# A graph network layer on one core: the order of the last table stores, the register loads and one late-turned group

## The chip, the cores and the metric

The kernel runs on one core of a Trainium2 chip. The metric is the device time of one execution in microseconds. A profiled execution is slower than the ones that are timed; it is used to see what happens, and the timed runs to say how long it takes.

## The reference

There are N = 6250 nodes with H = 128 features and E = 100000 edges, sorted by destination, with four attributes each. Everything is float32.

```
msg_in     = concat([x[src], x[dst], edge_attr], axis=1)      # E x 260
h          = silu(msg_in @ mW1 + mb1)                          # E x 128
messages   = h @ mW2 + mb2
aggregated = segment_sum(messages, dst)                        # N x 128
u          = silu(concat([x, aggregated]) @ uW1 + ub1)
updated    = u @ uW2 + ub2
r          = layer_norm(x + updated) * ln_g + ln_b
out        = normalize(x + r)                                  # a second norm, without weights
```

## The kernel before

**Tables.** The first matmul is split by the rows of mW1. A table A = x @ mW1[:128] and a table B = x @ mW1[128:256] + mb1 are computed once for all nodes and stored to HBM as tab_a and tab_b. This is the prologue's loop (from L367): the nodes come in seven parts k = 0 to 6 of eight tiles of 128 (part 6 has one tile, so its two stores have 64 KB, the others 512 KB). In each part TensorE turns the next part of x (turn_x, L336), multiplies (L377), ScalarE copies A out of PSUM (L379), VectorE adds the bias to B (L380), and SyncE stores first A (L383), then B (L384). Each part's last matmul is kept in the list `table`. The PSUM tiles come from a pool of four, all called "wide". A tile with zeros fills the rows of B behind the last node (L332 to L334).

**Edges.** The edges come in NG = 98 groups g of 1024 edges, eight tiles of 128. For each group:

- fetch(g) (L273): GpSimd gathers the rows of the edges' sources with one indirect DMA per tile (L277), up to eight of 64 KB per group. Groups 0 to 4 (below RAW = 5) gather from x itself, because A is not ready; the later ones from tab_a. A gather can be told to wait for matmuls named in the call: `fetch(4, *table[3:])` makes the first half of group 4 wait for the last matmul of part 3, the second half for that of part 4. The gathered rows lie in six buffers, so group 6 needs the buffer of group 0.
- load(g) (L598): SyncE loads mv, the 96 rows of B from the group's base node on (L604, with the base in a register of SyncE), and st, the four attribute rows of ea_d (L605). Every fourth group it also loads `near` for four groups from near_d (destinations, L315).
- node_matrix(g) (L607): VectorE makes a one-hot matrix of destinations in the upper 96 rows of st.
- products(g) (L632): TensorE multiplies st by mv (L636). For groups below RAW the gathered rows of x must be multiplied by mW1 too (L639), and for that they have been turned (transposed) before, by turn_rows (L357): eight transposes on TensorE and one copy of 128x1024 on VectorE (L362).
- hidden(g) (L645): VectorE adds the gathered rows of A and the products (L653, not for groups below RAW), ScalarE takes silu (L654).
- by_nodes(g) (L670): TensorE sums the edges by node with a second one-hot matrix (L665); add(g) (L676) adds the result on VectorE at the group's base, which needs the base in a register of VectorE.

Each engine works through its own queue in the order in which the code is written. In iteration g of the loop (L693) stand load(g+4), hidden(g), products(g+2), node_matrix(g+3), edge_matrix(g+1), add(g-2), by_nodes(g) and a fetch. The fetches of the start are fetch(5) behind turn_rows(2), with no matmul to wait for in its first half; fetch(6) with its second half behind products(0); fetch(7) and (8) in iterations 0 and 1; fetch(9) in iteration 3 behind products(4) and (5). From g = 12 on, group g+2 is fetched in iteration g, its second half behind the first sum of group g.

**What the change touches.** load_bases(g) (L343) loads the bases of 14 groups into registers of both SyncE and VectorE; it is called at k = 4 for the first 14. At k = 4 stand also fetch(4), destinations(0) and turn_rows(1). After the parts, groups 2, 3 and 4 are turned (L404 to L406), a tile `pad` of zeros is made and stored behind the last attribute in ea_d (L407 to L410), and the pools of the tables are closed. The buffers stbuf (L596) take memory that the tables had.

Of the kernel before, what the change touches and what calls it, by code (L numbers as in the profile page):

```python
# [8 lines left out]
F32 = mybir.dt.float32  # L9
# [5 lines left out]
ENG = mybir.EngineType  # L15
PSUM = bass.MemoryType.PSUM
DRAM = bass.MemoryType.DRAM

P = 128
# [5 lines left out]
def kernel(  # L25
# [40 lines left out]
    nc = tc.nc  # L66
    N, H = x.shape
# [3 lines left out]
    NP = NT * P  # L71
# [38 lines left out]

    tables = ExitStack()
    tpool = tables.enter_context(tc.tile_pool(name="tables", bufs=1, side="right"))
    tables_ps = tables.enter_context(tc.tile_pool(name="tables_ps", bufs=4, space=PSUM))

    def wide():
        return tables_ps.tile([P, G, P], F32, name="wide")

    def narrow():
        return wide()[:, :2, :].rearrange("p i f -> p (i f)")
# [148 lines left out]
    rows, bases, near = {}, {}, {}  # L268

    def tiles_of(g):  # L270
        return min(G, -(-(E - g * GE) // P))
# [57 lines left out]
    def by_node(t):  # L329
        return t[:NP].rearrange("(i p) f -> p i f", p=P)  # L330

    zeros = tpool.tile([W, H], F32, name="zeros")  # L332
    nc.vector.memset(zeros, 0.0)
    nc.sync.dma_start(tab_b[NP:NW], zeros)  # L334

    def turn_x(i0, n):  # L336
        pt = wide()
# [2 lines left out]
        nc.scalar.copy(xT[:, i0 * P : (i0 + n) * P], pt[:, :n, :].rearrange("p i f -> p (i f)"))  # L340
        return ins

    def load_bases(g):  # L343
        _, vals = nc.values_load_multi_w_load_instructions(
            base_i[0:1, g : g + RB],
            engines=(ENG.SP, ENG.DVE),
            min_val=0,
            max_val=NP,
            skip_runtime_bounds_check_because=IN_RANGE,
        )  # L350
        for k, v in enumerate(vals):
            bases[g + k] = v

    parts = groups(NT, G)
    table = []

    def turn_rows(g):  # L357

        px = wide()
        for i in range(G):  # L360
            ins = nc.tensor.transpose(px[:, i, :], rows[g][:, i, :], ident)
        nc.vector.tensor_copy(rows[g], px)  # L362
        return ins
# [3 lines left out]
    for k, (i0, n) in enumerate(parts):  # L367
        if k + 1 < len(parts):
            turn_x(*parts[k + 1])

        tb = x_sb[:, i0 : i0 + n, :]
        ta = tpool.tile([P, G, H], F32, name="t", bufs=2)
        for j0, m in groups(n, G // 2):
            pm = wide().rearrange("p (i s) f -> p i s f", s=2)
            for j in range(m):
                cols = slice((i0 + j0 + j) * P, (i0 + j0 + j + 1) * P)
                ins = nc.tensor.matmul(pm[:, j], xT[:, cols], w1, start=True, stop=True)  # L377
            own = slice(j0, j0 + m)
# [4 lines left out]
        nc.sync.dma_start(by_node(tab_a)[:, i0 : i0 + n, :], ta[:, :n])  # L383
        nc.sync.dma_start(by_node(tab_b)[:, i0 : i0 + n, :], tb)  # L384
# [12 lines left out]
        cols = slice(i0 * P, NW if i0 + n == NT else (i0 + n) * P)  # L397
        nc.vector.memset(acc[:, cols], 0.0)
        if k == 4:
            fetch(4, *table[3:])  # L400
            destinations(0)
            load_bases(0)
            turn_rows(1)
    fetch(RAW, None, turn_rows(2))  # L404
    for g in range(3, RAW):
        turn_rows(g)  # L406
    if E < NG * GE:  # L407
        pad = tpool.tile([ED, NG * GE - E], F32, name="pad")
        nc.vector.memset(pad, 0.0)
        nc.sync.dma_start(ea_d[:, E:], pad)  # L410
    tables.close()

    fixed = edges.enter_context(tc.tile_pool(name="fixed", bufs=1, space=PSUM))
# [8 lines left out]
    def node_y():  # L422
        return node_ps.tile([P, BT, H], F32, name="y")
# [171 lines left out]
    nodes = edges.enter_context(tc.tile_pool(name="nodes", bufs=1))  # L595
    stbuf = [held.tile([K1, GE], F32, name=f"st{k}") for k in range(NST)]  # L596

    def load(g):  # L598

        if g % NQ == 0 and g:  # L600
            destinations(g)
        if g % RB == 0 and g:
            load_bases(g)
        nc.sync.dma_start(mv[g % NM][:W], tab_b[bass.ds(bases[g], W), :])  # L604
        nc.sync.dma_start(stbuf[g % NST][W:], ea_d[:, g * GE : (g + 1) * GE])  # L605

    def node_matrix(g):  # L607

        nc.vector.tensor_scalar(  # L609
            stbuf[g % NST][:W],  # L610
            near.pop(g),
            p_next,
            0.0,
            op0=OP.is_equal,
            op1=OP.add,
            accum_out=deg_q[g // DQ % 2][:, g % DQ * 32 : g % DQ * 32 + 1],
        )
# [13 lines left out]

    def products(g):  # L632
        pre = rows_ps()
        st = stbuf[g % NST].rearrange("k (i c) -> k i c", i=G)
        for i in range(tiles_of(g)):
            ins = nc.tensor.matmul(pre[:, i, :], st[:, i, :], mv[g % NM], start=True, stop=g >= RAW)  # L636
            begun.setdefault(g, ins)
            if g < RAW:
                ins = nc.tensor.matmul(  # L639
                    pre[:, i, :], rows[g][:, i, :], w1[:, 0, :], start=False, stop=True  # L640
                )
            ended[g] = ins
        return pre
# [26 lines left out]
    def by_nodes(g, h, oh):  # L670

        pt = degrees(g)
        sums(g, pt, h, oh, 0, tiles_of(g))
        return pt

    def add(g, pt):  # L676
        at = acc[:, bass.ds(bases[g], W)]
        nc.vector.tensor_add(at, at, pt[:, :W])  # L678
        if g % DQ == 0:
            for k in range(min(DQ, NG - g)):  # L680
                row = slice(32 * k, 32 * k + 1)
                at = deg[row, bass.ds(bases[g + k], W)]
                nc.vector.tensor_add(at, at, pt[row, W:])  # L683

    for g in range(LEAD):
        load(g)
# [5 lines left out]
    fetch(6, None, ended[0])  # L692
    for g in range(NG):  # L693
        if g == 1:
            load_weights()
        if g == 2:
            running.append(destination_checks(node_y()))
        if g == 8:
            running.append(fuse_weights())
        for c in range(1, NC):  # L700
            if g == max(1, c * EC // GE - 10):
                attributes(c)
            if g == max(1, c * EC // GE - 10) + 1:
# [12 lines left out]
        if g - 2 in pt:  # L716
            add(g - 2, pt.pop(g - 2))
        if last:
            break
        pt[g] = by_nodes(g, h.pop(g), oh.pop(g))  # L720
        if CLOSE <= g + 2 < NG:
            fetch(g + 2, begun[g + 2], summing[g])
        elif g == 0:
            fetch(7, ended[1], begun[2])
        elif g == 1:
            fetch(8, begun[3], summing[1])
        elif g % 2:
            fetch(g // 2 + 8, ended[g + 1], begun[g + 2] if g == CLOSE - 3 else ended[g + 2])
        if g >= NG - 3:
            add(g - 1, pt.pop(g - 1))  # L730
        for i0, n, first in batches[:-1]:
            if g == (first if first >= NG - 3 else first + 1):
                fine = i0 == batches[-2][0]
                running.append(node_batch(i0, n, *node_tiles(nodes, node_y), fine=fine))
        for _ in range(0 if g == NG - 2 else 4 if g == NG - 3 else 2 if g >= NG - 6 else 1):
            advance(running)
        if g == NG - 3:
            final = node_batch(
                *batches[-1][:2],
                nodes,  # L740

                lambda name, p=P: gath.tile([P, G, H], F32, name="ga")[:p, :BT],
                lambda: rows_ps()[:, :BT],
                final=True,
            )
            next(final)
        if g == NG - 2:
            next(final)
# [195 lines left out]
```

## Time and profile before

| | us |
|---|---|
| median of three timed runs | 1005.5 |
| lowest and highest of them | 1005.47, 1007.06 |
| the profiled execution | 1170.27 |
| its span, from the first to the last instruction | 1168.2 |

| engine | busy us | share of the span |
|---|---|---|
| TensorE matmuls | 741.4 | 63% |
| TensorE weight loads | 672.5 | 58% |
| VectorE | 486.6 | 42% |
| ScalarE | 238.1 | 20% |
| GpSimd | 742.1 | 64% |

The TensorE clock that was granted in the profiled execution is 0.673 in the mean. In a timeline a line gives the start in us, the duration in us, the engine (PE is TensorE, DVE VectorE, ACT ScalarE, POOL GpSimd, SPq the queue of DMAs that SyncE issues), the line of the code, the operation, what it writes and reads, and in brackets how long the engine was idle before and what ended that. A DMA's line covers its issue, not its transfer. In a table by stretches each row gives the stretch, its length, busy time with a count of instructions for PE, weight loads, DVE, ACT and POOL, the granted clock, the share of the DMA engines and GB/s. In the page's list of groups a line ends with busy time and mean ns, and behind the second bar the idle time before it.

### The profile page before, as it was taken

To read this page: it belongs to the slowest core of one execution; us is meant where nothing else is said; L and a number is where in the kernel's file an instruction comes from. 1 tells how busy PE (TensorE), PEld (TensorE's weight loads), DVE (VectorE), ACT (ScalarE), POOL (GpSimd) and SP (SyncE) were. 2 spreads that over 40 slices of the span, in tenths; PEclk is the share of its full clock that TensorE was granted. 3 is DMA by queue.
4 is the path that set the end of the run, shared out by engine and by line. 5 is a ranking of instruction groups with operands and counts; after the bars stand their busy time and mean duration, and the time that the engine had idled before them with its cause. 6 is when DMAs were issued, how large, how long until landed. Compare 5 with 4: busy or idle time off the path is not lost.

```text
span 1168.2 us, 11310 instructions
## 1 busy us (share of the span) xinstructions
PE 741.4 (63%) x3645; PEld 672.5 (58%) x3645; DVE 486.6 (42%) x1019; ACT 238.1 (20%) x296; POOL 742.1 (64%) x790
## 2 busy tenths in 40 slices
PE   5776886665666667647656756676566555764663
PEld 4665775655655565546555655665465545664552
DVE  4461754432523532542443343353252343254354
ACT  1210121220311120221121122032121113022233
POOL 6646666666666566656666666666666666666661
PEclk9777887666577567666666666566656766656677
DMA  8762232232222231223132223232322222222220
GB/s 197 202 162 71 76 83 63 67 82 63 72 67 74 56 80 51 74 70 82 48 83 60 70 59 82 63 80 59 76 66 71 73 59 68 70 53 65 55 70 25
DMA packets 70076, 89.01 MB, mean 76 GB/s; under 512 B 20703, under 2 KB 51694, under 8 KB 70010
## 3 DMA queue, kind: packets, MB, share of 16 engines
q0 software_dynamic: 25024, 51.30, 17.9%
q1 hardware_dynamic: 40408, 35.03, 10.4%
q10 hardware_dynamic: 4578, 1.89, 0.7%
q8 instruction: 31, 0.51, 0.2%
q14 instruction: 35, 0.29, 0.1%
HBM read 76.78 MB, written 11.38 MB: 75 GB/s over the span
## 4 chain that ended last, share of the span: by engine, by line
issue 34%; PE 31%; POOL 23%; DVE 2%; another core or an unknown queue 2%; DMA 1%; ACT 1%; DVEq 0%; POOLq 0%; SPq 0%; ACTq 0%
POOL ga L277 23%; PE pre L636 15%; PE pt L665 12%; PE y L533 1%; DMA ga<-tab_a,src_i 1%; PE pre L639 1%; PE y L524 1%; PE y L510 1%; PE y L514 0%; PE y L518 0%; DVE s L653 0%; PE pt L660 0%; ACT L654 0%; DVE st L483 0%
## 5 line engine op out<-in xcount | busy, mean ns | idle before, releaser
L277 POOL DMA_INDIRECT ga<-tab_a,src_i x742 | 702.7, 947 | 384.5 <-issue 204.1
L636 PE MATMUL pre<-mv,st 100*128 100x128 f32 x1564 | 342.1, 393 | 228.3 <-issue 200.6
L636 PEld LDWEIGHTS pre<-mv,st 100*128 100x128 f32 x1564 | 312.6, 298 | 248.5 <-issue 228.6
L665 PE MATMUL pt<-oh,h 128*128 128x96 f32 x1564 | 293.6, 346 | 149.2 <-issue 148.0
L665 PEld LDWEIGHTS pt<-oh,h 128*128 128x128 f32 x1564 | 279.4, 264 | 166.5 <-issue 164.4
L653 DVE TENSOR_TENSOR s<-ga,pre 128x1024 f32<-128x1024 f32 x92 | 112.2, 1220 | 500.5 <-DMA ga<-tab_a,src_i 425.5
L654 ACT ACTIVATE h<-s 128x1024 f32<-128x1024 f32 x92 | 97.1, 1056 | 665.0 <-issue 438.8
L609 DVE TENSOR_SCALAR_CACHE_REDUCE st<-near,p_next 96x1024 f32<-96x1024 uint8 x98 | 124.3, 1269 | 3.1 <-DMA near<-near_d 1.5
L622 DVE TENSOR_TENSOR oh<-w_row,rel 128x768 f32<-128x768 f32 x98 | 93.0, 949 | 42.1 <-remote 34.3
L535 DVE TENSOR_TENSOR y<-y,xs 128x512 f32<-128x512 f32 (+1 forms) x12 | 8.3, 688 | 79.1 <-issue 76.1
L277 POOL DMA_INDIRECT ga<-in_x_dram,src_i x32 | 30.7, 959 | 16.5 <-issue 8.5
L654 ACT ACT_TABLE_LOAD x23 | 29.5, 1283 | 24.2 <-PE pre L639 17.7
L377 PE MATMUL wide<-w,xT 128*128 128x256 f32 x98 | 29.0, 460 | 6.1 <-DVE x_sb L380 6.1
L489 ACT ACT_TABLE_LOAD x24 | 30.8, 1283 | 6.1 <-DVE mv L484 5.7
L521 ACT ACTIVATE uT<-y,ub_col 128x512 f32<-128x512 f32 (+1 forms) x12 | 8.1, 678 | 105.9 <-remote 74.5
L377 PEld LDWEIGHTS wide<-w,xT 128*128 128x128 f32 x98 | 22.7, 238 | 10.7 <-DVE x_sb L380 6.8
L533 PEld LDWEIGHTS y<-u,uT 128*128 128x128 f32 x94 | 22.7, 327 | 10.2 <-issue 10.2
L678 DVE TENSOR_TENSOR acc<-acc,pt 128x96 f32 x98 | 23.7, 242 | 5.3 <-remote 4.5
L533 PE MATMUL y<-u,uT 128*128 128x128 f32 x94 | 25.2, 416 | 0.0
L683 DVE TENSOR_TENSOR deg<-deg,pt 1x96 f32 x98 | 24.4, 249 | 1.0
L639 PE MATMUL pre<-w,ga 128*128 128x128 f32 x80 | 19.7, 326 | 4.5 <-issue 4.3
L524 PE MATMUL y<-ub_row,ones 1*128 1x512 f32 (+1 forms) x24 | 14.9, 704 | 8.8 <-ACT uT L521 8.8
(118 smaller groups left out, 358.3 us busy)
## 6 DMA issues: line engine op xcount, KB each, us to landing
ga<-tab_a,src_i POOLq DMA_INDIRECT x742
near<-near_d SPq DMA_DIRECT2D x24, 384.0 KB
mv<-tab_b SPq DMA_DIRECT2D x98, 48.0 KB
tab_a<-t SPq DMA_DIRECT2D x6, 512.0 KB
tab_b<-x_sb SPq DMA_DIRECT2D x6, 512.0 KB
xs<-in_x_dram SPq DMA_DIRECT2D x11, 256.0 KB
out_dram<-z SPq DMA_DIRECT2D x11, 256.0 KB
st<-ea_d SPq DMA_DIRECT2D x98, 16.0 KB
```

Source lines behind the costliest of these rows:

```text
L277: ins = nc.gpsimd.indirect_dma_start(out=rows[g][:, i, :], out_offset=None, in_=x if g < RAW else tab_a[:, :], in_offset=bass.IndirectOffs ...
L377: ins = nc.tensor.matmul(pm[:, j], xT[:, cols], w1, start=True, stop=True)
L489: nc.scalar.activation(r[:, :n], mv[:, :n, 1], AF.Sqrt, bias=eps)
L524: nc.tensor.matmul(y[:, :n], ones[0:1, :], ub2_row[:, None, :].to_broadcast([1, n, H]), start=True, stop=False,)
L533: nc.tensor.matmul(y[:, i, :], by_p[:, :, i], u2, start=final, stop=final or i == n - 1)
L609: nc.vector.tensor_scalar(stbuf[g % NST][:W], near.pop(g), p_next, 0.0, op0=OP.is_equal, op1=OP.add, accum_out=deg_q[g // DQ % 2][:, g % D ...
L622: nc.vector.tensor_tensor(oh, w_row[:, None, :].to_broadcast([P, G, W]), rel[:, g, :, None].to_broadcast([P, G, W]), op=OP.is_equal,)
L636: ins = nc.tensor.matmul(pre[:, i, :], st[:, i, :], mv[g % NM], start=True, stop=g >= RAW)
L639: ins = nc.tensor.matmul(pre[:, i, :], rows[g][:, i, :], w1[:, 0, :], start=False, stop=True)
L653: nc.vector.tensor_add(s[:, :n], ga[:, :n], ps[:, :n])
L654: nc.scalar.activation(h[:, :n], s[:, :n], AF.Silu)
L665: ins = nc.tensor.matmul(pt[:, :W], h[:, i, :], oh[:, i, :], start=i == 0, stop=i == tiles_of(g) - 1)
```

## The change

Five things, none of which changes the arithmetic:

- The store of B of part 5 is held back until part 6, so the order is A5, A6, B5, B6.
- The zeros behind B and behind the attributes are stored in the prologue's beginning, both from the still zero tile deg. The tiles zeros and pad and their memsets go.
- load_bases is called for one engine at a time: for SyncE at k = 4, for VectorE in iteration 1 of the loop, into a dictionary of its own, which add() reads.
- destinations(0) moves from k = 4 to k = 3, and fetch(4) from k = 4 to k = 5, where it waits for the matmuls of parts 4 and 5.
- Group 4 is no longer turned ahead of the loop but in iterations 0 and 1, in two halves of four tiles, each with a PSUM tile of the node stage. The st buffers of groups 0 and 1 come from the pool "work". The pool of PSUM tiles is closed by itself.

```diff
-    zeros = tpool.tile([W, H], F32, name="zeros")
-    nc.vector.memset(zeros, 0.0)
-    nc.sync.dma_start(tab_b[NP:NW], zeros)
+
+    nc.sync.dma_start(tab_b[NP:NW], deg[:W, :H])
+    if E < NG * GE:
+        nc.sync.dma_start(ea_d[:, E:], deg[:ED, : NG * GE - E])
...
-    def load_bases(g):
+    def load_bases(g, engine, bases):
...
-            engines=(ENG.SP, ENG.DVE),
+            engines=(engine,),
...
-        nc.sync.dma_start(by_node(tab_b)[:, i0 : i0 + n, :], tb)
+        stores.append((by_node(tab_b)[:, i0 : i0 + n, :], tb))
+
+        while stores and k != len(parts) - 2:
+            nc.sync.dma_start(*stores.pop(0))
...
             turn_rows(0)
+            destinations(0)
...
         if k == 4:
-            fetch(4, *table[3:])
-            destinations(0)
-            load_bases(0)
+            load_bases(0, ENG.SP, bases)
             turn_rows(1)
+        if k == 5:
+            fetch(4, *table[4:])
     fetch(RAW, None, turn_rows(2))
-    for g in range(3, RAW):
+    for g in range(3, RAW - 1):
         turn_rows(g)
-    if E < NG * GE:
-        pad = tpool.tile([ED, NG * GE - E], F32, name="pad")
-        nc.vector.memset(pad, 0.0)
-        nc.sync.dma_start(ea_d[:, E:], pad)
+    st_first = [work.tile([P, GE], F32, name="s")[:K1] for _ in range(2)]
+    tables_ps.close()
     tables.close()
...
+    st = {g: st_first[g] if g < 2 else stbuf[g % NST] for g in range(NG)}
...
-            load_bases(g)
+            load_bases(g, ENG.SP, bases)
+            load_bases(g, ENG.DVE, at_bases)
...
-        at = acc[:, bass.ds(bases[g], W)]
+        at = acc[:, bass.ds(at_bases[g], W)]
...
+    def turn_late(g):
+
+        for lo in range(0, G, BT):
+            px = node_y()
+            for i in range(BT):
+                nc.tensor.transpose(px[:, i, :], rows[g][:, lo + i, :], ident)
+            yield
+            nc.vector.tensor_copy(rows[g][:, lo : lo + BT], px)
...
     for g in range(NG):
         if g == 1:
+            load_bases(0, ENG.DVE, at_bases)
             load_weights()
...
+        if g == 0:
+            late = turn_late(RAW - 1)
+            next(late)
         if g + 2 < NG:
             pre[g + 2] = products(g + 2)
...
         pt[g] = by_nodes(g, h.pop(g), oh.pop(g))
+        if g < 2:
+            next(late, None)
```

More of the change, by code (lines that the diff above doesn't have):

```diff
@@ L112 @@
     tpool = tables.enter_context(tc.tile_pool(name="tables", bufs=1, side="right"))
-    tables_ps = tables.enter_context(tc.tile_pool(name="tables_ps", bufs=4, space=PSUM))
+    tables_ps = ExitStack()
+    tables_pool = tables_ps.enter_context(tc.tile_pool(name="tables_ps", bufs=4, space=PSUM))
     def wide():
-        return tables_ps.tile([P, G, P], F32, name="wide")
+        return tables_pool.tile([P, G, P], F32, name="wide")
     def narrow():
@@ L267 @@
     near_d = dram.tile([NG, GE], U8, name="near_d")
-    rows, bases, near = {}, {}, {}
+    rows, near = {}, {}
+    bases, at_bases = {}, {}
     def tiles_of(g):
@@ L354 @@
     parts = groups(NT, G)
-    table = []
+    table, stores = [], []
     def turn_rows(g):
@@ L602, in load @@
         if g % RB == 0 and g:
-            load_bases(g)
+            load_bases(g, ENG.SP, bases)
+            load_bases(g, ENG.DVE, at_bases)
         nc.sync.dma_start(mv[g % NM][:W], tab_b[bass.ds(bases[g], W), :])
-        nc.sync.dma_start(stbuf[g % NST][W:], ea_d[:, g * GE : (g + 1) * GE])
+        nc.sync.dma_start(st[g][W:], ea_d[:, g * GE : (g + 1) * GE])
     def node_matrix(g):
         nc.vector.tensor_scalar(
-            stbuf[g % NST][:W],
+            st[g][:W],
             near.pop(g),
@@ L633, in products @@
         pre = rows_ps()
-        st = stbuf[g % NST].rearrange("k (i c) -> k i c", i=G)
+        st_g = st[g].rearrange("k (i c) -> k i c", i=G)
         for i in range(tiles_of(g)):
-            ins = nc.tensor.matmul(pre[:, i, :], st[:, i, :], mv[g % NM], start=True, stop=g >= RAW)
+            ins = nc.tensor.matmul(pre[:, i, :], st_g[:, i, :], mv[g % NM], start=True, stop=g >= RAW)
             begun.setdefault(g, ins)
@@ L681, in add @@
                 row = slice(32 * k, 32 * k + 1)
-                at = deg[row, bass.ds(bases[g + k], W)]
+                at = deg[row, bass.ds(at_bases[g + k], W)]
                 nc.vector.tensor_add(at, at, pt[row, W:])
+    def turn_late(g):
[5 more added lines that the diff above has]
+            nc.vector.tensor_copy(rows[g][:, lo : lo + BT], px)
     for g in range(LEAD):
```

## The prediction

> **What bounds the kernel now.** I read the page's costliest groups, then GpSimd's own timeline, then the chain of waits at the start, then SyncE's and VectorE's timelines there, then the DMA rate by stretches.
>
> ```profile
> L277 POOL DMA_INDIRECT ga<-tab_a,src_i x742 | 702.7, 947 | 384.5 <-issue 204.1
> L277 POOL DMA_INDIRECT ga<-in_x_dram,src_i x32 | 30.7, 959 | 16.5 <-issue 8.5
> ```
>
> Each gather keeps GpSimd busy 947 ns, and 0.30 us pass before the next can start: 1.25 us. There are 742 + 32 + the 8 of group 0 = 782, so 977.5 us. The first starts at 3.07. The last:
>
> ```profile
> 1146.39 0.94 POOL L277 DMA_INDIRECT ga<-tab_a,src_i  x1 [0.30 <-issue]
> ```
>
> It ends at 1147.3; 20.9 us of tail follow to the span's end at 1168.2. So the profiled span is 3.07 + 977.5 + 20.9 = 1001.5 plus 166.7 us of gaps between gathers, most of them in the loop behind a TensorE at a granted clock of 0.673. The profiled execution took 1170.27, 2.07 more than its span. The median of the runs shown is 1005.5; less 2.07 that is 1003.4, so those runs leave about 2 us for all gaps, perhaps 6 if their tail is 4 us shorter. Hence the loop's stalls are mostly missing from them, GpSimd issues almost without a break, and a microsecond by which the gathers start earlier is a microsecond of the total. That is the assumption on which everything below stands. The gaps that the change can touch lie ahead of the loop:
>
> ```profile
> 59.18 0.94 POOL L277 DMA_INDIRECT ga<-in_x_dram,src_i  x1 [0.30 <-issue]
> 69.81 0.94 POOL L277 DMA_INDIRECT ga<-tab_a,src_i  x1 [9.69 <-DMA tab_a<-t]
> ...
> 78.54 0.95 POOL L277 DMA_INDIRECT ga<-tab_a,src_i  x1 [0.30 <-issue]
> 81.65 0.94 POOL L277 DMA_INDIRECT ga<-tab_a,src_i  x1 [2.16 <-PE pre L639]
> ```
>
> The reader is to see two gates one after the other. Group 5, the first from table A, waits until A has landed (69.81). Group 6 then waits for TensorE's first products, which free its buffer (81.65; without that wait it would start at 69.81 + 10.0 = 79.8). What counts for the total is the later gate. The products start at 73.44, when their operands have landed:
>
> ```profile
> 65.64 3.42 DVE L362 COPY ga<-wide 128x1024 f32<-128x1024 f32 x3
> 69.07 0.35 DVE L409 MEMSET pad<- 4x352 f32 x1
> ```
>
> ```profile
> 64.30 0.38 SPq L384 DMA_DIRECT2D tab_b<-x_sb  x1
> 64.77 1.18 SPq L383 DMA_DIRECT2D tab_a<-t  x1
> 66.00 1.25 SPq L384 DMA_DIRECT2D tab_b<-x_sb  x1
> 69.45 0.31 SPq L410 DMA_DIRECT2D ea_d<-pad  x1
> 70.08 0.36 SPq L604 DMA_DIRECT2D mv<-tab_b  x1
> 70.81 0.27 SPq L605 DMA_DIRECT2D st<-ea_d  x1
> ```
>
> ```profile
> 69.45 1.30 DMA ea_d<-pad
> ```
>
> ```profile
> 57.50:60.00 2.50, 2.50 (x7) 2.02 (x6) 0.65 (x2) 0.00 (x0) 1.89 (x3) 0.50 1.04 307
> 64.50:68.50 4.00, 1.47 (x14) 1.23 (x12) 4.00 (x6) 0.00 (x0) 0.00 (x0) 1.00 0.98 286
> 68.50:69.00 0.50, 0.00 (x0) 0.00 (x0) 0.50 (x1) 0.00 (x0) 0.00 (x0) 0.81 0.28 78
> 69.00:69.50 0.50, 0.00 (x0) 0.00 (x0) 0.49 (x3) 0.00 (x0) 0.00 (x0) 0.50 0.00 0
> ```
>
> (The last two columns are the DMA share and GB/s.) The last stores (A5, B5 of 512 KB, A6, B6 of 64 KB) run at 286 GB/s and are moved by about 68.7. SyncE then issues the pad, which waits for VectorE's three copies and a memset; only then mv for group 0, and its st waits 1.30 us for the pad to land. From the issue of st to the first product are 73.44 - 70.81 = 2.63 us, and from there to group 6 are 8.2.
>
> **The change, part by part.**
>
> *B5 and B6 behind A6.* A6 no longer queues behind 524 KB: 524/286 = 1.83 us earlier. B's own end does not move: the same bytes.
>
> *Pad and zeros stored early, from deg.* Two small DMAs at about 20 us (the zeros' issue there took 0.34), with 20 us of slack; the two memsets (0.17 and 0.35) go. At the end, mv no longer waits for the pad: it can go when B has landed. Transfers stop between 68.5 and 69.0; a store's completion reaches the waiting engine later, so I bound it by 69.2 and 69.9: mv is 0.2 to 0.9 earlier, and I take 0.75 as the rate is nearest to zero at 68.7. st follows mv by 0.37 (71.27 to 71.64 for the next group) instead of 0.73: another 0.36. The Trainium skill, "DMA: Bandwidth & Descriptors" ("Anatomy of one DMA", told there of the GpSimd path), puts about 2.0 us of fixed cost on a DMA, most of it the receipt of the write; by that the pad's wait would be 0.7 us longer than the row's 1.30, and the gain as much larger. The row decides: 0.36.
>
> *near for groups 0 to 3 loaded at k = 3.* 393 KB, or 1.37 us at 286 GB/s, leave the stretch of A4, B4 and A5 (issue at 57.58) for the lull after 48 us, where the rate between 50 and 56 is 44 GB/s. SyncE now waits there for near_d to land; behind it is A4, which in the trace isn't ready before 56.25, so the wait lies in slack. In the profile this buys nothing: transfers stop at 63.5 and A5 is issued at 63.57. But A5 is that late because TensorE ran the matmuls of part 5 at half clock (0.57 over 56 to 63: 6.83 us for 18, against 3.32 of weight loads for 16 at full clock). Without TensorE's stalls A5 would come some 3.4 us sooner, into a queue that is full until 63, and then the 1.37 count in full. The timed runs have few of those stalls, so I count 1.37; the other end is 0.
>
> *Gathers of group 4 behind table[4] and table[5].* The second half moves from 55.4 to after the last matmul of part 5, about 62.8, and ends at 68. A5 to B6 now share the engines with it. The Trainium skill, same page, section "Issuing engines are not separate DMA queues", says that transfers of all engines run on the same 16 and interleave; this speaks against the change. By it alone 262 KB cost 262/286 = 0.92 us on B. The row of 57.5 to 60, stores with gathers beside them, has 307 GB/s against 286 without: gathers ask for 65.5 KB per 1.25 us, 52 GB/s, of which 21 came on top, so 60% displaces: 0.55 us on B, 0.4 on A (three gathers). I take the row. GpSimd is free for group 5 at 68.0, before A has landed in any of the cases in which A6 gains under 1.8; if it gains more, everything there is earlier with it.
>
> *Registers apart.* VectorE's loads at k = 4 are the 1.85 us "issue" ahead of the copy at 59.99. They move to g = 1, where VectorE has gaps (9.16 busy of 12 us from 68 to 80) and node matrix 4 waits 1.46 us for near anyway. Behind them are node matrix 4 and edge matrix 2, needed by products 4 and sums 2, over 8 us later. Nothing, both ways, as long as TensorE's queue is behind: at worst 1.85.
>
> *Group 4 turned in the loop; st of groups 0 and 1 in work.* One of three copies (1.14) leaves VectorE's queue ahead of the loop; with the pad and the registers that is 3.3 us, so node matrix 0 (70.96 to 72.24) moves clear of the operands. Eight transposes go into the first two iterations: 8 x 0.116 (2.78 for 24) = 0.93 us of TensorE, and two half copies on VectorE. TensorE is some ten microseconds ahead of the gathers' gates there: group 8 is due at 81.65 + 20 and needs products 3. Cost nothing; if that cover is gone, 0.93 and more (third rival).
>
> **Sum.** First gate, table A: 1.83 + 1.37 - 0.4 = 2.8 earlier. Second gate, products 0: 0.75 + 0.36 + 1.37 - 0.55 = 1.93 earlier. Before, the second was later by 81.65 - 79.8 = 1.85; after, by 2.7. So **the second gate decides and the gain is 1.9 us**: against the profiled execution 1170.27 - 1.9 = 1168.4 if its stalls stayed as they were, which I don't expect; against the median **1003.5 us**. The ends of the terms give 0.0 (near 0, mv 0.2, gathers -0.55) to 2.5 (pad by the longer wait).
>
> **The rivals.**
>
> 1. *The products are not the gate in the timed runs.* TensorE's own rows begin the last matmuls of products 0 at 79.70, well over a microsecond before their release shows; the 0.43 us per two matmuls are half clock. If the release is that much quicker unprofiled, table A gates, and the whole 2.8 or a little more counts: 1002.6. For it: the gap budget of 2 to 6 us. Against it: ScalarE is released at the same 81.45.
>
> 2. *Hidden.* The near load was no burden in the timed runs either and B's landing is pushed back by group 4's gathers: 0.36 + 0.2 - 0.55 = 0.0: 1005.5.
>
> 3. *Slower: products 4.* Group 9's gathers wait for the products of group 4 (in the profile from 114.6 to 116.95, 2.34 us, on L639). These now need the late turn: two half copies behind register loads, a node matrix and an edge matrix on VectorE (1.85 + 1.27 + 0.95) plus 0.93 of transposes: 5.0 us at worst on that path, less the 1.9 won: 1008.6. It decides once products 4 end later than 81.65 + 30 = 111.6. In the profile TensorE crawled from 90 to 104 and they did; without the crawl I count 81.4 + 2.4 + 3.8 + 1.8 + 3.6 + 1.8 + 3.6 = 98.4, so 13 us of slack.
>
> **How the numbers follow.** A measurement here tells 0.2%, 2.0 us, from no change. The forecast has 52% with a range of its own of 1002.8 to 1004.6, half of it on either side of 1003.5; rival 1 has 24%, all faster; rival 2 has 14%, same; rival 3 has 10%. Faster 0.25 + 0.24 = 0.49, same 0.27 + 0.14 = 0.41, slower 0.10. The range for 8 in 10 takes in rival 2 and most of rival 1: 1001.5 to 1005.9.
>
> **What would show it.** In the profile of the changed kernel: A6's issue ahead of B5's; the first gather from tab_a less than 7 us after the end of part 5's matmuls instead of 7.0; no pad at 69; mv and st of group 0 issued 0.4 apart; the wait of group 6's first gather on products 0 longer than 2.16, not shorter; eight transposes by tens of nanoseconds between the first products. I am wrong if group 6's wait shrinks or goes (rival 1), if st of group 0 is no nearer to A5's issue than the 7.24 us of before (rival 2), or if group 9 waits for products 4 in runs without TensorE's crawl (rival 3).

## The result, and the profile after

The changed kernel takes 1000.89 us (median of four runs, 1000.09 to 1001.25), the kernel before beside it 1006.28 (1005.47 to 1008.05). The ratio is 0.994 with an interval of 0.9924 to 0.9955: faster, by 5.4 us in the medians and 6.0 (4.5 to 7.6) by the ratio. The forecast had the direction and the frame of two gates, but 1003.5 us, and its range ended at 1001.5.

In some sessions TensorE stands still in the loop for a reason that the profile doesn't show, in either kernel, as in the profile before (1170 us); runs of such a session are compared only with the kernel before of the same session. The profile of the changed kernel was free of it: that execution took 1001.0 us, as long as the timed ones, so the profiler by itself costs nothing that shows here. So that like is set beside like, the unchanged kernel was profiled once more (1007.67 us, the run b_same). The waits of TensorE, the total in us, how often and the longest, in the profile before:

```profile
PE pre L636 <- issue: 200.6, 95, 6.8
```

and in b_same:

```profile
PE pre L636 <- issue: 37.2, 10, 4.7
```

"Issue" is a wait for nothing that the profile shows; 163 us of it are gone, and the span falls from 1168.2 to 1005.6. From here on "before" in timelines is b_same.

**GpSimd's gathers.** The group of the 742 gathers from table A on the page, busy and idle, before and changed (the code's lines shifted; L277 is now L279, L361/L362 are L364/L365, L383 and L384 are L386 and L390, L604 and L605 are L612 and L613, L636 and L639 are L644 and L647):

```profile
L277 POOL DMA_INDIRECT ga<-tab_a,src_i x742 | 700.6, 944 | 232.4 <-issue 189.9
```

```profile
L279 POOL DMA_INDIRECT ga<-tab_a,src_i x742 | 700.8, 944 | 226.1 <-issue 207.9
```

Busy and idle together are 933.0 and 926.9: 6.1 us less, all in the second number. Its place is seen in GpSimd's timelines. Before:

```profile
52.37 0.94 POOL L277 DMA_INDIRECT ga<-in_x_dram,src_i  x1 [0.31 <-issue]
59.40 0.94 POOL L277 DMA_INDIRECT ga<-tab_a,src_i  x1 [6.09 <-DMA tab_a<-t]
...
69.82 0.94 POOL L277 DMA_INDIRECT ga<-tab_a,src_i  x1 [0.73 <-PE pre L639]
```

Changed:

```profile
54.18 0.94 POOL L279 DMA_INDIRECT ga<-tab_a,src_i  x1 [0.30 <-issue]
...
64.17 0.94 POOL L279 DMA_INDIRECT ga<-tab_a,src_i  x1 [0.30 <-issue]
...
979.84 0.95 POOL L279 DMA_INDIRECT ga<-tab_a,src_i  x1 [0.30 <-issue]
```

A gather always has 0.30 idle ahead of it, so before 5.79 us were lost ahead of group 5 and 0.43 ahead of group 6, 6.2 in all, which covers the difference of 6.1. In the changed kernel neither gate holds anything. Its gathers run from 3.06 to 980.79, which is 782 times 1.25, and 18.2 of tail make the span of 999.0. Between the gathers nothing is left to win at the start.

**The chain behind the second gate.** SyncE's timeline before:

```profile
45.89 0.38 SPq L383 DMA_DIRECT2D tab_a<-t  x1
...
52.56 2.50 SPq L383 DMA_DIRECT2D tab_a<-t  x1
55.12 0.94 SPq L384 DMA_DIRECT2D tab_b<-x_sb  x1
59.53 0.32 SPq L410 DMA_DIRECT2D ea_d<-pad  x1
60.16 0.36 SPq L604 DMA_DIRECT2D mv<-tab_b  x1
60.89 0.27 SPq L605 DMA_DIRECT2D st<-ea_d  x1
```

and VectorE's:

```profile
53.44 2.29 DVE L362 COPY ga<-wide 128x1024 f32<-128x1024 f32 x2
57.91 1.23 DVE L362 COPY ga<-wide 128x1024 f32<-128x1024 f32 x1 [2.19 <-PE wide L361]
59.15 0.35 DVE L409 MEMSET pad<- 4x352 f32 x1
```

The third copy, that of group 4, stands alone: it waits for TensorE's transposes, and these for the rows of group 4, which GpSimd gathers until 53.31, into queues full of stores (DMA share 1.01 from 54 to 57.3 us). Behind it are the memset, the pad's store, mv, st and products 0, which start at 63.54. SyncE's timeline of the changed kernel:

```profile
43.45 0.38 SPq L386 DMA_DIRECT2D tab_a<-t  x1
...
48.62 0.99 SPq L386 DMA_DIRECT2D tab_a<-t  x2
49.70 1.80 SPq L390 DMA_DIRECT2D tab_b<-x_sb  x2
55.17 0.36 SPq L612 DMA_DIRECT2D mv<-tab_b  x1
55.63 0.43 SPq L613 DMA_DIRECT2D s<-ea_d  x1
```

and TensorE's:

```profile
57.71 0.77 PE L644 MATMUL pre<-mv,s 100*128 100x128 f32 x2 [8.29 <-DMA s<-ea_d]
...
67.07 0.60 PE L698 MATMUL y<-ident,ga 128*128 128x128 f32 x4
```

A5 and A6 go out as one pair, B5 and B6 as the next; mv waits for B alone. Products 0 start at 57.71 and end at 63.66, half a microsecond ahead of group 6. The late transposes (67.07, 0.60 for four) lie beyond.

### The profile page after: what moved, and what is told of

Its sections match the earlier page's. It is cut to its first block, busy times and chain, and to the rows that moved or that the text cites. A ratio compares the mean times of both kernels' runs of the same rounds, so it can differ in the third digit from the quotient of the medians.

```text
span 999.0 us, 11309 instructions
## 1 busy us (share of the span) xinstructions
PE 678.5 (68%) x3645; PEld 625.0 (63%) x3645; DVE 486.4 (49%) x1018; ACT 239.0 (24%) x296; POOL 740.6 (74%) x790
## 4 chain that ended last, share of the span: by engine, by line
POOL 38%; issue 26%; PE 17%; DMA 14%; DVE 4%; ACT 0%; DVEq 0%; ACTq 0%; POOLq 0%; SPq 0%
POOL ga L279 38%; DMA ga<-tab_a,src_i 12%; PE pre L644 8%; PE pt L673 4%; DVE s L661 2%; PE wide L380 1%; PE pre L647 1%; DMA x_sb<-in_x_dram 1%; PE y L538 1%; PE wide L342 1%; DMA w<-in_L_gnn_mW_dram 0%; DMA tab_b<-x_sb 0%; PE y L529 0%; DMA ga<-in_x_dram,src_i 0%; PE y L515 0%
## 5 line engine op out<-in xcount | busy, mean ns | idle before, releaser
L279 POOL DMA_INDIRECT ga<-tab_a,src_i x742 | 700.8, 944 | 226.1 <-issue 207.9
L644 PE MATMUL pre<-mv,st 100*128 100x128 f32 x1532 | 318.0, 389 | 278.7 <-DVE s L661 239.3
L644 PEld LDWEIGHTS pre<-mv,st 100*128 100x128 f32 x1532 | 292.0, 291 | 300.7 <-DVE s L661 259.1
L673 PE MATMUL pt<-oh,h 128*128 128x96 f32 x1564 | 254.6, 333 | 5.8 <-DVE deg L691 3.1
L673 PEld LDWEIGHTS pt<-oh,h 128*128 128x128 f32 x1564 | 253.2, 253 | 8.2 <-issue 2.9
L279 POOL DMA_INDIRECT ga<-in_x_dram,src_i x32 | 30.8, 962 | 9.8 <-issue 7.6
L380 PE MATMUL wide<-w,xT 128*128 128x256 f32 x98 | 22.8, 387 | 0.2 <-DVE rel L201 0.2
L380 PEld LDWEIGHTS wide<-w,xT 128*128 128x128 f32 x98 | 18.7, 196 | 2.8 <-DVE rel L201 0.4
L489 DVE BATCH_NORM_AGGREGATE mv<-st 128x2 f32<-128x6 f32 x98 | 17.8, 182 | 3.4
L578 ACT ACTIVATE z<-z,shift,r 128x128 f32<-128x128 f32 x47 | 19.2, 479 | 0.0
L553 DVE SCALAR_TENSOR_TENSOR z<-y,r,xs 128x128 f32<-128x128 f32 x47 | 16.5, 351 | 1.7
L550 DVE SCALAR_TENSOR_TENSOR y<-y,mv,g_b 128x128 f32<-128x128 f32 x47 | 16.5, 351 | 1.2
```

The lines of the kernel that those rows point to most:

```text
L279: ins = nc.gpsimd.indirect_dma_start(out=rows[g][:, i, :], out_offset=None, in_=x if g < RAW else tab_a[:, :], in_offset=bass.IndirectOffs ...
L644: ins = nc.tensor.matmul(pre[:, i, :], st_g[:, i, :], mv[g % NM], start=True, stop=g >= RAW)
L673: ins = nc.tensor.matmul(pt[:, :W], h[:, i, :], oh[:, i, :], start=i == 0, stop=i == tiles_of(g) - 1)
```

## The experiments

Two theories stand against each other. **G, two gates in series:** group 5 waits for table A, group 6 for products 0 (its buffer), and GpSimd loses time at whichever is later; a part of the change that moves one gate wins only until the other holds. **O, one gate:** table A alone gives the gain, and the rest of the change is hidden. A kernel beginning with b is the kernel before with one part of the change done alone, one with a is the changed kernel with one part undone. "Lost" is idle time ahead of a gather less 0.30.

### The two halves alone

Order alone (b_order_3):

```diff
-        nc.sync.dma_start(by_node(tab_b)[:, i0 : i0 + n, :], tb)
+        stores.append((by_node(tab_b)[:, i0 : i0 + n, :], tb))
+        while stores and k != len(parts) - 2:
+            nc.sync.dma_start(*stores.pop(0))
```

> The kernel before with the order of the last stores alone (part 6's A part ahead of the B parts of parts 5 and 6). If two gates act (table A, then group 6's buffer behind products 0), table A comes some 2 to 3 us earlier, but zeros, st and near load still stand where they were, products 0 start no earlier than 62.5, and the gap moves from group 5 to group 6: the gain is under 1.5 us, 1005 to 1006.5 where before gives 1006.5. If table A alone decides, the gain is 2.5 us or more, 1004 or less.

Measured: 1007.29 us against 1008.62, ratio 0.9991 (0.9982 to 1.0). GpSimd's timeline:

```profile
53.95 0.95 POOL L277 DMA_INDIRECT ga<-tab_a,src_i  x1 [0.30 <-issue]
...
67.08 0.94 POOL L277 DMA_INDIRECT ga<-tab_a,src_i  x1 [3.44 <-PE pre L641]
```

TensorE's:

```profile
61.48 0.77 PE L638 MATMUL pre<-mv,st 100*128 100x128 f32 x2 [5.61 <-DMA mv<-tab_b]
```

Group 5 waits for nothing any more, and group 6 waits 3.14 too long for products 0. The gap has moved from the first gate to the second. O's prediction of 2.5 us or more fails. Products 0 start at 61.48, where the expectation had 62.5 at the earliest: in this execution the whole table part was earlier (A4 at 42.50, not 45.89).

Late turn alone (b_late_1), with the zeros still stored at the end of the prologue:

```diff
-    for g in range(3, RAW):
+    for g in range(3, RAW - 1):
...
+        if g == 0:
+            late = turn_late(RAW - 1)
+            next(late)
...
+        if g < 2:
+            next(late, None)
```

> The kernel before with the fifth raw group turned inside the loop by halves, and nothing else of the change. If it lets the zeros go out and with them mv, st and products 0 some 2 to 3 us earlier (the wait for the fourth group's late rows is off the chain), but table A still opens at 59, then the gap ahead of group 5 stays near 5.8 us and only the 0.4 ahead of group 6 goes: gain under 1 us. If the late turn carries a gain of its own, 2 us or more.

Measured: 1005.19 against 1006.37, ratio 0.9991 (0.9981 to 1.0). GpSimd's timeline:

```profile
57.15 0.94 POOL L277 DMA_INDIRECT ga<-tab_a,src_i  x1 [3.39 <-DMA tab_a<-t]
```

and SyncE's:

```profile
50.73 2.65 SPq L383 DMA_DIRECT2D tab_a<-t  x1
53.43 0.94 SPq L384 DMA_DIRECT2D tab_b<-x_sb  x1
54.47 0.35 SPq L410 DMA_DIRECT2D ea_d<-pad  x1
56.80 0.36 SPq L604 DMA_DIRECT2D mv<-tab_b  x1
```

The mirror image: group 6 loses nothing, products 0 start at 59.73, and 3.09 are lost to table A. The expectation had a gap near 5.8; it is shorter because the table part was earlier here too (A4 at 43.90): counted from A4, group 5 comes after 13.25 us, and after 13.51 in b_same. The pad leaves at 54.47, right behind B6, and mv doesn't come until 56.80, when by the profile B has landed: without the third copy ahead of it the pad costs mv nothing here. Each half is worth 0.9 us by the ratio (0 to 1.8), at the edge of what can be told; the whole change is worth 6.0.

### Each part undone

Late turn undone (a_late_4): group 4 is turned ahead of the loop again.

```diff
-    for g in range(3, RAW - 1):
+    for g in range(3, RAW):
...
-            late = turn_late(RAW - 1)
-            next(late)
```

> The changed kernel with group 4 turned ahead of the loop again. On chips where TensorE stalls, group 6 was released 8 to 10 us later than in the changed kernel and the end was the same. Where before takes 1006: theory G (two gates): no gap ahead of group 5, one ahead of group 6 of 1 to 3 us behind products 0, and 1002 to 1004 us. Theory O (table A alone counts): 1000.9.

Measured: 1003.43 against 1006.34, ratio 0.9966 (0.9951 to 0.998). It keeps 3.4 of the 6.0 that the ratio of 0.994 is worth, so the late turn is worth about 2.6, give or take 2 (2.5 by the medians). VectorE's timeline:

```profile
56.91 1.23 DVE L365 COPY ga<-wide 128x1024 f32<-128x1024 f32 x1 [3.32 <-DMA ga<-tab_a,src_i]
...
58.34 1.27 DVE L617 TENSOR_SCALAR_CACHE_REDUCE s<-near,p_next 96x1024 f32<-96x1024 uint8 x1
```

TensorE's:

```profile
59.82 0.77 PE L644 MATMUL pre<-mv,s 100*128 100x128 f32 x2 [2.95 <-DVE s L617]
```

GpSimd's:

```profile
65.96 0.94 POOL L279 DMA_INDIRECT ga<-tab_a,src_i  x1 [1.79 <-PE pre L647]
```

Here there is no pad, and the copy hurts all the same: node_matrix(0) stands behind it in VectorE's queue and starts at 58.34 instead of 52.46, products 0 wait for it, and 1.49 are lost ahead of group 6. The next run, a_order_5, can be set beside it: there the tables came at the same time (A4 at 44.67, here 44.79) and st was issued at the same time (56.35, here 56.37), but group 4 is turned late, and products 0 start at 58.31 and not at 59.82, 1.51 earlier. Another 0.71 were lost ahead of group 4, whose first half waits for part 4's matmuls; that belongs to the late table part of this execution and not to the turn.

Order undone (a_order_5):

```diff
-        while stores and k != len(parts) - 2:
+        while stores:
```

> The changed kernel with A's and B's last parts stored alternately again (part 5's B part ahead of part 6's A part). If the earlier run of part 6's A part is what gave most of the 5.4 us (table A decides), the time goes back by 2.5 us or more, to 1003.4 or later, with a gap of 2.5 us or more ahead of group 5's first gather. If group 6's buffer decides and this order moves only the first gate, products 0 stand where they stood and the time stays within 1 us of 1000.9; group 5's gap is under 1.5 us and is taken out again at group 6.

Measured: 1003.66 against 1006.52, ratio 0.9975 (0.9964 to 0.9986), so the order is worth about 3.5 of the 6.0, give or take 2 (2.5 by the medians). GpSimd's timeline:

```profile
56.23 0.94 POOL L279 DMA_INDIRECT ga<-tab_a,src_i  x1 [2.25 <-DMA tab_a<-t]
```

1.95 are lost there and none ahead of group 6; up to 1.22 of them are the later table part of this execution (A4 at 44.67, and 43.45 in the changed kernel's profile). The expectation had given O this outcome; read with b_order_3 it is G's as well, since the second gate is out of the way in this kernel. What I wrote for G, that only a fraction would show, was wrong: with the second gate lifted, the first has no cover.

Near load undone (a_near_2): destinations(0) back at k = 4.

> The changed kernel with the near load of the first two groups back ahead of part 5's A part. If its 384 KB lie in the full queue as the forecast had it (1.37 us), table A opens later by 1 to 1.5 us and the time goes back by 0.5 to 1.5 us, with a gap of that size ahead of group 5. If the near load is hidden (the queue takes it beside other work), the time stays within 0.5 us of 1000.9 and no gap shows.

Measured: 1004.39 against 1007.86, ratio 0.997 (0.9958 to 0.9981). GpSimd's timeline:

```profile
54.50 0.95 POOL L279 DMA_INDIRECT ga<-tab_a,src_i  x1 [0.75 <-DMA tab_a<-t]
...
65.58 0.95 POOL L279 DMA_INDIRECT ga<-tab_a,src_i  x1 [1.37 <-PE pre L647]
```

0.45 and 1.07 are lost, 1.5 together, at both gates as the near load stands ahead of both; mv is issued 13.26 behind A4, 1.54 later than the 11.72 of the changed kernel. By the ratio the near load is worth 3.0, give or take 2 (1.9 by the medians); what is beyond 1.5 shows in no gap of this profile, while its 742 gathers took 702.2 us instead of 700.8 for their own part. So the near load counts, in the size that the forecast gave it (1.37) or more.

### The kernel before again

> The kernel before, unchanged, profiled once more, to see it without TensorE's stalls. The changed kernel's gathers run from 3.06 to 979.84 us without one gap, so the 5.4 us that it gained must be gaps here. Theory A (table A is the gate): one gap of about 5.4 us ahead of group 5, released by the landing of tab_a, and group 6 starts 10.0 us after group 5 with no gap. Theory P (the recorded prediction's: products 0 are the gate): group 6's first gather has a gap of some 1.8 us of its own, released by the products, and the gap ahead of group 5 is correspondingly smaller, 3.5 us. Span about 1004 if the stalls are absent, some 1168 if they come again.

Measured: 1007.67 us in its one execution, 1007.01 beside it; its lines are shown above.

### Sessions in which TensorE stalls

Twelve of the runs fell in such sessions; they are told here with what they can still show. The edits are those above; a_same is the changed kernel as it is, a_pad_1 is the changed kernel with the pad stored at the end again:

```diff
-    if E < NG * GE:
-        nc.sync.dma_start(ea_d[:, E:], deg[:ED, : NG * GE - E])
...
+    if E < NG * GE:
+        pad = tpool.tile([ED, NG * GE - E], F32, name="pad")
+        nc.vector.memset(pad, 0.0)
+        nc.sync.dma_start(ea_d[:, E:], pad)
```

> The kernel before with the order of the last stores alone (A5, A6, B5, B6). In the unstalled profile of before, group 5 starts at 59.40 (gap 6.09, table A) and group 6 at 69.82, 0.43 late, right at the end of products 0 (69.7). Theory G (two gates, the later decides): A lands earlier and the gap ahead of group 5 shrinks by 1.8 us or more, but group 6 still waits for products 0, which start at about 63.5 as before; its gap grows by as much and the time stays: 0.0 to -0.4 us. Theory O (table A is the only gate that counts): -1.8 us by the bytes of B5, up to -3.8 us by the 7.8 us from A5's issue to group 5 in before against less than 4 in the changed kernel.

> The changed kernel with the order undone (A5, B5, A6, B6). Its gathers run without a gap now: group 5 starts at 54.18 with tables landed, group 6 at 64.17, with products 0 ending at about 63.7. Both theories: A6 lands 1.8 us later or more, so a gap of 1 to 2.5 us opens ahead of group 5, and the time rises by the same. Theory G adds that products 0 do not move (B's bytes end when they did), so group 6 has no gap of its own.

> The changed kernel with group 4 turned ahead of the loop again (its gathers stay behind parts 4 and 5). Theory G: the last turn waits for the gathers of group 4, which land some 3 to 5 us after their issue at 49 to 53; VectorE's copy and then node matrix 0 come after it, products 0 start 1.3 to 3 us later, group 6 gets a gap of 1 to 2.5 us and the time rises by that. Theory O: group 5 is untouched, 0.0 us.

> The changed kernel with the near load of groups 0 to 3 back at k = 4, behind B4. 393 KB at some 290 GB/s, 1.4 us, come ahead of A5, and SyncE is 1.1 us later at its register loads and A5. Theory G: both gates 1.1 to 2.4 us later, of which 0.4 (group 6) to 1 (group 5) is slack: +0.7 to +2.0 us. If the load is hidden as in the stalled profile: 0.0.

> The changed kernel with the order undone (A5, B5, A6, B6), once more, because on the chip of the first try TensorE stalled all through the loop (1160 us for before too) and hid the start. On a chip where before takes some 1006: group 5 gets a gap of 1 to 2.5 us ahead of it, group 6 none of its own, and the time is 1 to 2.5 us above the changed kernel, so 3 to 4.5 below before. If TensorE stalls again, within 1 us of before.

> The changed kernel with group 4 turned ahead of the loop again, once more on what may be another chip. Theory G (two gates): group 5 without a gap, group 6 with one of 1 to 2.5 us, since products 0 now wait for the landing of group 4's gathers, their turn and the copy; the time rises over the changed kernel by that. Theory O (table A alone counts): nothing.

> The changed kernel with group 4 turned ahead of the loop again, third chip. Where TensorE stalls in the loop (two chips so far), it was 5 to 8 us slower than before itself: group 5 without a gap, group 6 with one of 12 us behind products 0. Where it doesn't, theory G (two gates): products 0 wait for the landing of group 4's gathers, their turn and the copy; group 6 gets a gap of 1 to 3 us and the time rises by that over the changed kernel. Theory O (table A alone counts): 0.0.

> The changed kernel as it is, beside before on the same chip. Where TensorE doesn't stall: 5.4 us below before (1000.9 to 1006.3), no gap between gathers. Where it does (before at 1160): the gates of the start are earlier by some 6 us, but the loop's gathers wait for TensorE in every second group, so the start's gain is won only as far as TensorE's own work starts earlier: 0 to 6 us below before.

> The changed kernel with the order undone (A5, B5, A6, B6). Where before takes 1006: a gap of 1 to 2.5 us ahead of group 5 by both theories, none at group 6, 1002 to 1003.4 us. If A6 had that much slack, 1000.9. Where before takes 1160 or more, the end says nothing about the start (group 6 8 to 10 us later gave the same end).

> The kernel before with the order of the last stores alone. Where before takes 1006: theory G: group 5 earlier by 1.8 us or more, group 6 held by products 0 at the same place, total -0.4 to 0.0 us. Theory O: -1.8 to -3.8 us.

> The changed kernel with the order undone (A5, B5, A6, B6). Where before takes 1006: a gap of 1 to 2.5 us ahead of group 5, none at group 6 beyond it, 1002 to 1003.4 us. If A6 had that much slack, or if products 0 hold group 6 at the same place anyway, 1000.9. Where before takes 1160 or more the end says nothing about the start.

> The changed kernel with the pad set to zero and stored at the end of the table's part again, ahead of mv and st. The forecast gave the early zeros 0.75 us for mv and 0.36 us for st, 1.11 us on products 0; by that the time goes back by 0.7 us or more, to some 1001.6 to 1002, with a gap ahead of group 6. If what held the pad back before was VectorE's copy of the fourth group (waiting for late rows), then with that copy gone to the loop the pad is issued right behind B's parts, lands beside them, and nothing changes: within 0.5 us of 1000.9, no gap at group 6.

| run | us | before, same session | ratio, interval | idle ahead of group 5, group 6 |
|---|---|---|---|---|
| b_order | 1159.04 | 1160.95 | 0.9984 (0.9972 to 0.9996) | 6.38, 2.08 |
| a_order | 1160.45 | 1160.95 | 0.9998 (0.9988 to 1.0007) | 2.58, 2.00 |
| a_late | 1168.06 | 1160.95 | 1.0046 (1.0028 to 1.0064) | 0.39, 12.33 |
| a_near | 1160.06 | 1160.95 | 0.9983 (0.9971 to 0.9995) | 1.78, 2.10 |
| a_order_2 | 1159.23 | 1161.59 | 0.9966 (0.9944 to 0.9989) | 2.13, 2.02 |
| a_late_2 | 1170.25 | 1161.59 | 1.0072 (1.0053 to 1.009) | 0.39, 12.10 |
| a_late_3 | 1177.91 | 1172.24 | 1.0037 (1.0011 to 1.0064) | 0.45, 14.30 |
| a_same | 1178.71 | 1172.24 | 1.0066 (1.0044 to 1.0088) | 1.01, 8.19 |
| a_order_3 | 1162.10 | 1161.52 | 0.9998 (0.9986 to 1.0011) | 2.10, 2.04 |
| b_order_2 | 1159.33 | 1161.52 | 0.9983 (0.9971 to 0.9994) | 6.57, 2.10 |
| a_order_4 | 1168.51 | 1170.57 | 0.9974 (0.9957 to 0.9992) | 2.15, 2.17 |
| a_pad_1 | 1165.29 | 1161.66 | 1.0029 (1.0012 to 1.0045) | 0.36, 8.25 |

In these sessions GpSimd waits in the loop for TensorE again and again (the kernel before had 166.7 us of such gaps in its first profile), but a later start is a later end here too. In the profiles of the session of 1160.95, group 6 starts at 78.62 (b_order), 74.29 (a_order), 87.64 (a_late) and 78.67 (a_near), and from there to the end of the span it takes 1078.6, 1080.2, 1080.4 and 1081.4 us: the starts differ by 13.4, the rest by 2.8. So these times do bear on G and O: with the late turn undone group 5 waits for nothing and group 6 for 12 us and more, and in the medians a_late and a_late_2 end 7.6 and 11.0 us behind a_order and a_order_2 of their sessions, in which group 5 does wait. By O they would end earlier. The order alone took the idle ahead of group 5 from 9.69 in the first profile to 6.38 and 6.57. The medians of a_late_3 and a_same, 0.8 apart, seem to say otherwise, but their profiled executions took 1182.24 and 1173.62 us, 8.6 apart, and group 6 starts there at 89.29 and 79.55; the runs of a_late_3 alone lie between 1167.37 and 1183.61.

What these sessions can't give is the size of a part. Even a_same, with nothing undone, has 8.19 ahead of group 6. The link is again a copy on VectorE:

```profile
71.05 1.23 DVE L365 COPY ga<-wide 128x1024 f32<-128x1024 f32 x1 [7.35 <-remote]
```

This is group 3's, whose transposes had ended by 57.7; products 0 follow at 73.96. In a_order that copy started at 61.87 after 0.40 of idle. What held it in a_same the profile doesn't name beyond "remote". Whether the early zeros are worth anything by themselves stays open in time: a_pad_1 fell here too, with 8.25 beside a_same's 8.19.

## Why the prediction was wrong

**The frame held.** GpSimd issues almost without a break, so an earlier start is an earlier end; two gates lie ahead of the loop, table A and then group 6's buffer. The unstalled profiles agree with this (6.2 lost at the gates, 6.1 less on the page), and b_order_3 and b_late_1 show the gates one behind the other. Rival 1 (table A alone) would have been nearer in time, 1002.6, and table A did hold the larger gap, 5.79 against 0.43; but by b_order_3 moving it alone gains 0.9 and not 2.8. Rival 2 (hidden) is refuted by the ratio. Rival 3 (products 4 and group 9) didn't occur: in the changed kernel's profile no gather behind group 5 loses more than a few hundredths of a microsecond. For the sessions in which TensorE stalls, a_same was 0.66% slower than before; the hold of VectorE's copy is seen there, its cause is not settled.

**The failing step is the sum's second gate, 1.93: the late turn was put at nothing, and the pad's gain at 0.75, where one copy on VectorE held both.** In the two unstalled profiles products 0 move from 63.54 to 57.71, 5.83 us:

- 2.44 of it is that the whole table part was later in b_same: A4 was issued at 45.89 there and at 43.45 in the changed kernel. This isn't the change: with the order alone, the same code up to A4 as before, it was 42.50, with the late turn alone 43.90, and in the kernels with a part undone 42.62 to 44.79. TensorE's granted clock between 36 and 42 us was 0.72 in b_same and in a_order_5 (A4 at 44.67) and 1.00 in the other five; what held a_late_4 (44.79) the profile doesn't show. So b_same's lost 6.2 is on the high side, as is its time, 1007.67 against a median of 1006.28.
- 2.55 is mv, 14.27 behind A4 before and 11.72 in the changed kernel. The forecast had 0.75 + 1.37 - 0.55 = 1.57. The late turn alone moves mv to 12.90 behind A4 (b_late_1), 1.37 where the forecast had 0.75 for the pad; the near load undone costs 1.54 (a_near_2), where it had 1.37.
- 0.27 is st behind mv (0.73 and 0.46); the forecast had 0.36.
- 0.57 is from st to products 0 (2.65 and 2.08); the forecast had nothing. The profile names a different releaser (mv before, st in the changed kernel), and no run takes this apart.

At equal A4 the second gate came 3.39 earlier instead of 1.93. That is more likely too little than too much: in b_order_3 A4 was 3.39 earlier than in b_same, but the third copy only 2.00 (55.91), since it waits for group 4's rows, which GpSimd gathers at its own pace. What the forecast missed is the third copy. In the profile that it worked from, the three copies stood back to back (the row of 65.64, 3.42 for three), as TensorE's matmuls of part 5 came so late there (half clock) that group 4's rows, gathered by 60.1, had landed when VectorE got to them. So "one of three copies (1.14) leaves" and "cost nothing" looked right for the late turn. Without those stalls the first two copies are done at 55.7 and the third waits until 57.91 for rows that land late. What the forecast put down to the pad hung mostly on that copy: b_late_1 shows that without it the pad is covered by B's landing, and a_late_4 that without the pad the copy still holds products 0, through node_matrix(0), by 1.5 us against a_order_5. The late turn was put at nothing; undone it cost 1.49 ahead of group 6, and 2.6 by the ratio, give or take 2.

**"Before, the second was later by 1.85"** was 0.43 in b_same, because table A's gate there was at 59.40 and products 0 took 6.2 us from start to release, not 8.2. With gates that close, both had to move for either to count, and the sum's "second gate decides" was right only by the terms that it had.

**The first gate, 2.8**, can't be read beyond a bound, as nothing waits for it any more: 13.51 behind A4 before, at most 10.73 in the changed kernel, so at least 2.78. Its ingredients fit, as far as they can be bounded behind A4: with the order alone group 5 comes after at most 11.45, so at least 2.06 earlier (1.83 forecast), and with the near load undone after 11.88, so at least 1.15 later than in the changed kernel (1.37 forecast). A6's own issue had a price that I hadn't put in: it took SyncE 2.50 us in b_same, 2.65 in b_late_1 and 1.37 in a_order_5, where A5 and A6 together take 0.99 when they go out ahead of B5. The gathers' share that I subtracted (0.4 and 0.55 for group 4 beside the stores) was not tested by itself; nor were the registers. Two sums are slightly off as they stand: 1005.5 - 1.93 is 1003.57, and the upper end with the longer wait for the pad is 1.93 + 0.7 = 2.6 and not 2.5.

**The budget of gaps** was 2 us with the tail of 20.9 and 6 with a shorter one. The tail measured 18.2, so the floor is a span of 999.0 and not 1001.5, and the 1003.4 of the runs shown left 4.4 for all gaps; the runs beside the changed kernel, 1006.28 less 2.0, left 5.3, and that is the gain measured. I leaned to 2 and so held a gain of more than 4 for almost excluded; my own arithmetic allowed it.

**What would show it.** Right: A6 ahead of B5, no pad at the end, mv and st 0.46 apart, the first gather from tab_a less than 7 us behind part 5's matmuls, but only just (6.9: ScalarE's copy behind them starts at 47.28, the gather at 54.18) and held by the gathers ahead of it and not by the table; st 7.01 behind A5's issue (9.59 in b_same); the eight transposes, in two rows of four with 0.43 us each until the next matmuls begin. Wrong: the wait of group 6, which was to be longer than 2.16 and is gone, though not for rival 1's reason: group 5's is gone too.

Not settled: at equal A4 the two profiles leave 3.8 us (5.79 - 2.44 + 0.43) while the medians have 5.4 and the ratio 6.0 (4.5 to 7.6). The start of the table part differs by up to 3.4 us between the unstalled profiles, and where neither gate holds, a short delay of it has room. How much of the rest that is, and how much is the third copy's own timing, one profile for each kernel can't tell.

## What to carry to other kernels

Where one engine issues without a break behind two gates, price each gate by its whole chain, down to what the last instruction in each queue waits for, and expect the parts not to add: here two halves were worth 0.9 us each alone by the ratio, the whole change 6.0, and undone the halves cost 2.6 and 3.5, give or take 2. The profiles show the same without that noise, as a gap that moves from one gate to the other. If the profile has stalls that the timed runs lack, operations that stand back to back in it may be waiting in the runs that count; work out the floor of the bounding engine from its own rows first and see how large a gain it leaves.

## What the runs showed of the hardware

- The issue of a DMA took SyncE longer when transfers lay ahead of it: 2.50 us (b_same) and 2.65 (b_late_1) for the 64 KB store A6 behind A5 and B5 of 512 KB, with the near load of 384 KB issued 5.5 us before; 1.37 (a_order_5) with the near load moved away; against 0.36 to 0.38 for A4 and A5 in b_same. What stands behind it on SyncE waits as well.
- A gather beside these stores can land later: between 40 and 56 us 4.1 to 4.8 us from issue to landing in b_order_3 (median 4.5), and up to 5.1 in b_same, though there the median was 2.5, as it is for the gathers of the whole loop.
- One and the same pair of kernels compares as 0.994 (1000.89 to 1006.28) in one session and as 1.0066 (1178.71 to 1172.24) in another, in which TensorE waits 218.6 us (a_same) for nothing that the profile shows; the same chip was seen both ways. Even so, in the session of 1160.95 the profiled executions took 1078.6 to 1081.4 us from group 6 to the end, whenever it started.
